# A transformer block in fp32: score beats paced by a weighted measure, and attention cut 5, 4 and 3 units ahead

## The chip, the cores and the metric

The kernel is one program on one core of a Trainium2 chip. The metric is device time in microseconds (us) of one launch, lower is better. Five engines work side by side, each through its own queue in order: PE (TensorE, matmuls), DVE (VectorE), ACT (ScalarE), POOL (GpSimd) and SP (SyncE, which here only issues DMAs). Semaphores tie them together: an instruction that waits holds up everything behind it on its engine.

## The reference

One pre-norm transformer layer in fp32 on x of shape (2, 1024, 1024), 32 heads of 32, feed-forward width 2752:

```python
def attn(x):
    qkv = x @ attn_qkvw + attn_qkvb            # q, k, v: 32 heads of 32
    scores = einsum('bhqd,bhkd->bhqk', q, k) / sqrt(32)
    ctx = einsum('bhqk,bhkd->bhqd', softmax(scores), v)
    return ctx @ attn_ow + attn_ob

def ffn(x):
    return (silu(x @ W_gate.T) * (x @ W_up.T)) @ W_down.T

x = x + attn(layernorm(x))
x = x + ffn(layernorm(x))
```

## The kernel before

**Stages.** There are two batches (b) and two blocks of 512 tokens in each (blk), so four blocks. The program is one long list of steps, nearly all of them one matmul each on PE:

- a head: layer norm, transposes and the first projections (`ln1`, `qk_steps`, `v_steps`);
- the fill: the remaining q, k and v projections of both batches (L370 and L432 are their matmuls);
- four times a rest (`rest(n)`), one for each block: the output projection (`oproj_steps`, matmul L770) with the second layer norm, then the feed-forward (`ffn_steps`): 22 chunks of gate and up products (`product`, matmul L912, a Strassen scheme of seven products), and after every fourth chunk a down projection.

A down projection (`down7`, matmul L1053, 28 matmuls of 512 columns) is again a Strassen scheme: each of its 14 accumulators in PSUM is added by DVE into one or two quarters of the residual x (L1066, L1068), 20 such adds in all, and DVE forms four sums of the hidden activations in between (`sums_h`, L1022 to L1028). The last, shorter part of a block uses `down` (matmul L985, add L996, and the regroupings `release`, L1010 and L1011). PSUM accumulators of all these, and the small transposes of attention, rotate through one pool of three buffers (tag `lin`).

**Attention.** It runs beside these steps in 64 units of two heads and 512 queries (`Unit`), 16 for each block. A unit has eight key tiles. Two key tiles at a time are scored by PE (`scores`, matmul L510) into two PSUM buffers (tag `s`, two of them). ACT copies each score tile to SBUF (L529), DVE keeps a running maximum over them (L526, one buffer `top`). After the eighth tile, DVE transposes and reduces the maximum (L549, L550), PE turns it (L564), DVE finishes it (L565), and DMAs through DRAM broadcast it to a tile m. Then for each key tile POOL subtracts the maximum (`less_maximum`, L580; every fourth on DVE in the first 16 units), ACT takes the exponential (L586), POOL or DVE adds neighbours (`add`, L596), and PE multiplies with the values (`values`, matmul L608), eleven beats or more after the score. The finished context goes to DRAM, and its softmax sums come back for a reciprocal on DVE (L696). Before the output projection of a block, POOL multiplies the context by these reciprocals (L718, waiting for the DMA of `rec`) and adds the bias to x (L762).

**What sets the order.** All instructions are written out in the order in which `Emitter.run` takes steps. It has a list `fill` (the projections, or a rest) and a list `paced` (attention). Each attention step with `beat=True` is a beat, eight for each unit, and every second one carries a pair of score tiles. A beat is held back until `due`, and `due` moves on by the work left divided by the beats left:

```python
                each = left / beats
                due = max(due, self.clock - each) + each
```

So beats lie evenly over the planned cost (`MM4 = 855.0` for one matmul of 512 columns) of the work in that call. If `fill` is not ready, `paced` goes on without regard to `due`. Steps with a delay (`em.later`) are written out when the planned clock has passed.

`attention_steps(cuts)` cuts the whole attention list, 512 beats and a drain of 14, into four lists. `lists[0]` is run beside the fill, `lists[1]` to `lists[3]` beside the rests of blocks 0 to 2; block 3 has none. Cuts stand at beats 144, 272 and 400: the fill takes the 16 units of the first block and two more, each later list 16 units. A rest keeps its last 30 matmuls (`late`) for the next call. On the side run the reloading of contexts (`prep_ctx`) and, during the fill, sums of weights on POOL (`weight_sum_steps`, L1164).

Of the kernel before, what the change touches and what calls it, by code (L numbers as in the profile page):

```python
# [24 lines left out]
class Steps:  # L25
# [3 lines left out]
    def __init__(self):  # L29
        self.items = []  # L30

    def add(self, fn, cost=0.0, needs=None, gives=None, beat=False):
        self.items.append((fn, cost, needs, gives, beat))

    def slack(self, cost):

# [2 lines left out]
    @property  # L39
    def cost(self):  # L40
        return sum(i[1] for i in self.items)


class Emitter:
# [21 lines left out]
    def run(self, fill, paced=None, side=()):  # L66

        paced = Steps() if paced is None else paced  # L70
        left = fill.cost + paced.cost
        beats = sum(i[4] for i in paced.items)
        due = self.clock

        def ready(q):
            return q.items and (q.items[0][2] is None or q.items[0][2] in self.done)

        while fill.items or paced.items:
            q = next((q for q in side if ready(q)), None)
            if q is None:  # L80
                go = ready(paced)
                if go and paced.items[0][4] and self.clock < due and ready(fill):
                    go = False
                q = paced if go else fill if ready(fill) else None
            if q is None:
                waiting = [p for p in self.put_off if p is not None]
                assert waiting, ("the steps wait for each other", fill.items[:1], paced.items[:1])
                self.clock = min(p[0] for p in waiting)
                self.settle()
                continue  # L90
            fn, cost, needs, gives, beat = q.items.pop(0)
            if beat:
                each = left / beats
                due = max(due, self.clock - each) + each
                beats -= 1
            fn()
            self.clock += cost
            if q is fill or q is paced:
                left -= cost
            if gives is not None:  # L100
                self.done.add(gives)
            self.settle()
# [28 lines left out]
def preln_block_kernel(  # L131
# [15 lines left out]
    B, S, H = x.shape  # L147
    G = w_qk.shape[0]
    KC = H // P
    NT = S // P  # L150
    NS = S // NH
# [7 lines left out]
    SCALE = 1.0 / math.sqrt(HD)  # L159
    MM4, MM1 = 855.0, 230.0  # L160
    UNITS = HEADS // 2
    QTR = 4
    LAG = 3
    RUN = 4
# [300 lines left out]
    class Unit:  # L465
# [4 lines left out]
        def __init__(self, n):  # L470
            self.n = n
            self.phase, u = divmod(n, UNITS)
            self.b, self.blk = divmod(self.phase, NS)
# [119 lines left out]
        def add(self, kt):  # L593

            eng = nc.vector if self.phase == 0 or kt % RUN == RUN - 1 else nc.gpsimd
            eng.tensor_tensor(self.p[kt], self.p[kt], self.p[kt - 1], ALU.add)  # L596
# [27 lines left out]
        def finish(self):  # L624
            part, n = divmod(self.u, UNITS // QTR)
            cs = Sm(f"cs_{self.name}")
# [11 lines left out]
    def attention_steps(cuts):  # L638


        units = [Unit(n) for n in range(B * NS * UNITS)]
        lists = [Steps()]
# [194 lines left out]
    def ffn_steps(q, b, blk, st, turn):  # L837
# [212 lines left out]
        def down7(pi, n, t, j):  # L1050
            if j == 0:
                st["pd"] = lps(f"pd{n}_{b}_{blk}_{pi}_{t}")
            nc.tensor.matmul(  # L1053
                st["pd"],
                lefts[n](pi)[:, j, t * P : (t + 1) * P],
                st["wp", pi, n, j],
                start=(j == 0),
                stop=(j == PART // 2 - 1),
            )
            if t == 1:  # L1060
                dst.next()
            if j == PART // 2 - 1:
                for (u, hf), op in goes[n]:
                    xs = st["x", t + u][:, hf * NH : (hf + 1) * NH]
                    if op == ALU.add:
                        nc.vector.tensor_tensor(xs, st["pd"], xs, op)  # L1066
                    else:
                        nc.vector.tensor_tensor(xs, xs, st["pd"], op)  # L1068

        def down_steps(pi):  # L1070
            if pi < WHOLE:
                for n in order:
                    for t in range(2):
                        for j in range(PART // 2):
                            q.add(lambda n=n, t=t, j=j: down7(pi, n, t, j), MM4)
                    if n in (1, 2, 4, 7):
                        q.add(lambda i=(1, 2, 4, 7).index(n): sums_h(pi, i))
                return


            for hf in range(NHF):
                for t in range(TB):
                    for ci in range(len(parts[pi])):
                        q.add(lambda hf=hf, t=t, ci=ci: down(pi, hf, t, ci), MM4)
                    if hf == 0 and t < 2:
                        q.add(lambda t=t: release(t))

# [100 lines left out]
    with tc.manual_schedule():  # L1188

        head, fill, keep_qk = Steps(), Steps(), Steps()  # L1190

        def two(fn, *args, **kw):

            q = Steps()
            fn(q, *args, **kw)
            return q

        def ln_steps(q, b, t0, t1, tools, ahead):

            load, norm, turn, _ = tools  # L1200
            for t in range(t0, t1):
                if t + ahead < t1:
                    q.add(lambda t=t + ahead: norm(t))
                turn(q, t)
                if t + 5 < NT:
                    q.add(lambda t=t + 5: load(t))

        tools = load, norm, turn, _ = ln1(0)
        for t in range(4):
            head.add(lambda t=t: load(t))  # L1210
        head.add(lambda: nc.sync.dma_start(bqk_t, b_qk))
        for _ in range(4):
            head.add(wst.next)
        head.add(lambda: load(4))
        for _ in range(8):
            head.add(dst.next)
        for _ in range(5):
            head.add(wst.next)
        head.add(lambda: norm(0))
        ln_steps(head, 0, 0, TB, tools, 1)  # L1220
        for _ in range(2):
            head.add(dst.next)
        qk_steps(head, 0, 0, [0])
        head.add(lambda: norm(TB))
        side = two(ln_steps, 0, TB, NT, tools, 1)
        head.items += merged(two(v_steps, 0, 0, range(TB)), side).items
        qk_steps(head, 0, 0, [1])

        v_steps(fill, 0, 0, range(TB, NT))
        for g in range(1, G // 2):  # L1230
            qk_steps(fill, 0, g)
        v_steps(fill, 0, 1)
        for g in range(G // 2, G - 2):
            qk_steps(fill, 0, g)

        tools = load1, norm1, turn1, stats1 = ln1(1)
        for t in range(5):
            fill.add(lambda t=t: load1(t))
        qk_steps(fill, 0, G - 2, [0])
        fill.items += merged(two(qk_steps, 0, G - 1, [0]), stats1(0, TB)).items  # L1240
        last = two(qk_steps, 0, G - 2, [1])
        qk_steps(last, 0, G - 1, [1])
        fill.items += merged(last, two(ln_steps, 1, 0, TB, tools, 1)).items
        fill.items += merged(two(v_steps, 1, 0, range(2)), stats1(TB, TB)).items
        fill.items += merged(
            two(v_steps, 1, 0, range(2, TB)), two(ln_steps, 1, TB, NT, tools, 1)
        ).items
        v_steps(fill, 1, 0, range(TB, NT))
        for g in range(0, G // 2):
            qk_steps(fill, 1, g)  # L1250
        v_steps(fill, 1, 1)
        for g in range(G // 2, G - 2):
            qk_steps(fill, 1, g)
        for s in range(NS):
            for g in range(G - 2, G):
                qk_steps(keep_qk, 1, g, [s])
            if s == 0:
                keep_qk.add(lambda: None, gives=("half", 1))

        def rest(n):  # L1260

            q, late, st = Steps(), Steps(), {}
            b, blk = divmod(n, NS)
            turn = oproj_steps(q, b, blk, st)
            ffn_steps(q, b, blk, st, turn)
            while late.cost < 30 * MM4:
                late.items.insert(0, q.items.pop())
            return q, late


        rests = [rest(n) for n in range(B * NS)]
        lists = attention_steps([(n + 1) * UNITS * NT + 2 * NT for n in range(B * NS - 1)])
        side = [*prep_ctx(0), *prep_ctx(1)]
        em.run(head)
        em.run(fill, lists[0], side=(*side, weight_sum_steps()))
        keep = keep_qk
        for (q, late), beats in zip(rests, [*lists[1:], None]):
            em.run(joined([keep, q]), beats, side=side)
            keep = late
        em.run(keep)  # L1280
        em.settle(True)
# [51 lines left out]
```

## Time and profile before

| | us |
|---|---|
| median of 3 runs (lowest, highest) | 3324.98 (3316.03, 3329.62) |
| the profiled execution's own time | 3320.48 |
| span of its trace | 3318.7 |
| PE busy | 3231.4 (97%) |
| DVE busy | 1904.9 (57%) |
| POOL busy | 1704.9 (51%) |
| ACT busy | 1431.9 (43%) |

Times below are us from the start of the span. The head and the fill end near 904; the rests of the four blocks follow. The matmuls of the last block's output projection begin at 2860.20, and beside it runs no attention. PE is busy nearly all the time, so time is lost where PE waits or where its clock is reduced: the list of waits (who waited for whom: total us, times, longest us), the table of windows (busy us and number of instructions of each engine in a stretch, PEclk being the granted share of PE's clock) and the timeline (start, length, instruction, and in brackets the idle time before it) are the views to read. The idle time of the other engines costs nothing by itself.

### The profile page before, as it was taken

How to read it: one execution, taken by the hardware profiler on the slowest of the kernel's cores; microseconds unless marked ns; L12 is line 12 of the kernel's file. 1: busy time of each engine (PE TensorE's matmuls, PEld its weight loads, DVE VectorE, ACT ScalarE, POOL GpSimd, SP SyncE). 2: the span in 40 equal slices, each digit the busy share in tenths (PEclk: the TensorE clock that was granted, in tenths of full speed). 3: DMA queues.
4: the chain of work that ended last, by engine and by line, in shares of the span. 5: the costliest groups of instructions: out<-in, count | busy, mean ns of one | idle time of the engine just before them, and what ended most of it. 6: DMA issues, size and time to landing. Idle time of an engine off the chain costs nothing. (4 is left out here: it accounts for less than half of the span.)

```text
span 3318.7 us, 44204 instructions
## 1 busy us (share of the span) xinstructions
PE 3231.4 (97%) x16576; PEld 1807.2 (54%) x16576; DVE 1904.9 (57%) x2462; ACT 1431.9 (43%) x1570; POOL 1704.9 (51%) x839
## 2 busy tenths in 40 slices
PE   8999999999999999998999999989999999999999
PEld 4444444444346555663465556634656566476775
DVE  2255565454366666667666676676666664344434
ACT  2244554444455555553555555545655554010000
POOL 0266666765675555557755565667665665200000
PEclk9999999999999999999999999999999999999999
DMA  4566666554534445546344454563454544544552
GB/s 154 173 184 203 211 197 208 187 178 137 148 101 139 146 146 147 148 142 199 103 134 144 138 143 136 149 179 118 135 145 145 146 139 138 177 145 152 154 153 95
DMA packets 337252, 507.33 MB, mean 153 GB/s; under 512 B 105360, under 2 KB 122000, under 8 KB 337040
## 3 DMA queue, kind: packets, MB, share of 16 engines
q1 hardware_dynamic: 280848, 405.91, 41.1%
q10 hardware_dynamic: 56192, 98.60, 9.8%
q8 instruction: 132, 2.16, 0.3%
q14 instruction: 80, 0.66, 0.1%
HBM read 429.14 MB, written 75.24 MB: 152 GB/s over the span
## 5 line engine op out<-in xcount | busy, mean ns | idle before, releaser
L580 POOL TENSOR_TENSOR p<-p,m 128x1024 f32<-128x1024 f32 x480 | 1172.0, 2464 | 27.3 <-DMA m<-d 27.2
L529 ACT COPY p<-s 128x1024 f32<-128x1024 f32 x512 | 516.6, 1012 | 908.1 <-DVE top L526 682.8
L526 DVE TENSOR_TENSOR top<-s,top 128x1024 f32<-128x1024 f32 x384 | 468.3, 1220 | 318.7 <-PE s L510 308.6
L912 PE MATMUL p<-sum,m 128*128 128x256 f32 x2688 | 619.7, 383 | 11.6 <-DVE gate L928 6.8
L586 ACT ACTIVATE p<-p 128x1024 f32<-128x1024 f32 x512 | 531.0, 1057 | 194.3 <-POOL p L580 177.7
L596 POOL TENSOR_TENSOR p<-p,p 128x1024 f32<-128x1024 f32 x96 | 227.6, 2371 | 678.7 <-ACT p L586 644.7
L912 PEld LDWEIGHTS p<-sum,m 128*128 128x128 f32 x2688 | 503.4, 190 | 133.2 <-issue 43.0
L912 PE MATMUL p<-xn2T,m 128*128 128x256 f32 x2016 | 473.1, 383 | 2.2 <-ACT gate L924 1.3
L370 PE MATMUL pq<-xnT,wqk 128*128 128x512 f32 x1024 | 465.2, 602 | 0.0
L1053 PE MATMUL pd<-wp,h 128*128 128x512 f32 x960 | 440.8, 605 | 11.4 <-DVE x L1066 10.9
L912 PEld LDWEIGHTS p<-xn2T,m 128*128 128x128 f32 x2016 | 377.6, 191 | 99.1 <-issue 45.1
L596 DVE TENSOR_TENSOR p<-p,p 128x1024 f32<-128x1024 f32 x160 | 273.0, 1706 | 121.7 <-ACT p L586 121.5
L370 PEld LDWEIGHTS pq<-xnT,wqk 128*128 128x128 f32 x1024 | 187.7, 191 | 253.6 <-issue 251.3
L1053 PEld LDWEIGHTS pd<-wp,h 128*128 128x128 f32 x960 | 178.3, 192 | 245.2 <-issue 207.0
L510 PE MATMUL s<-q,k 32*128 32x512 f32 x2048 | 298.6, 642 | 11.2 <-ACT p L529 11.2
L1066 DVE TENSOR_TENSOR x<-pd,x 128x512 f32<-128x512 f32 x360 | 236.8, 681 | 90.8 <-PE pd L1053 90.6
L608 PE MATMUL acc<-p,vals 128*32 128x256 f32 x4096 | 271.4, 382 | 3.5 <-DVE p L596 3.5
L1164 POOL TENSOR_TENSOR ws<-raw 128x512 f32<-128x512 f32 x62 | 88.5, 1428 | 337.7 <-DMA raw<-in_w_gu 184.1
L432 PE MATMUL pvv<-wv,xnT 128*128 128x512 f32 x512 | 232.9, 599 | 1.1 <-ACT xnT L266 1.1
L770 PE MATMUL po<-wo,ctx 128*128 128x512 f32 x512 | 231.8, 601 | 0.0
L608 PEld LDWEIGHTS acc<-p,vals 128*32 128x32 f32 x4096 | 119.8, 109 | 145.0 <-issue 71.2
L975 POOL MEMSET h<- 64x512 f32 x4 | 2.1, 518 | 340.9 <-PE pd L1053 340.9
(95 smaller groups left out, 2507.6 us busy)
## 6 DMA issues: line engine op xcount, KB each, us to landing
m<-dws SPq DMA_DIRECT2D x336, 256.0 KB
m<-in_w_gu SPq DMA_DIRECT2D x252, 256.0 KB
wp<-ddn SPq DMA_DIRECT2D x160, 256.0 KB
m<-d SPq DMA_DIRECT2D x64, 512.0 KB
wp<-in_w_dn SPq DMA_DIRECT2D x120, 256.0 KB
raw<-in_w_gu ACTq DMA_DIRECT2D x84, 256.0 KB
dws<-ws ACTq DMA_DIRECT2D x84, 256.0 KB
x<-in_x SPq DMA_DIRECT2D x32, 512.0 KB
```

What stands on the lines that cost most here:

```text
L370: nc.tensor.matmul(ps, wqk[b, g, w, hk][:, k, :], xnT[b, s][:, kc, :], start=(kc == 0), stop=(kc == KC - 1),)
L432: nc.tensor.matmul(st["ps"], xnT[b, t // TB][:, kc, (t % TB) * P : (t % TB + 1) * P], st["w"][kc], start=(kc == 0), stop=(kc == KC - 1),)
L510: nc.tensor.matmul(ps[a][:, h * NH : (h + 1) * NH], self.k[rows, i * P : (i + 1) * P], self.q[rows, :], start=True, stop=True,)
L526: nc.vector.tensor_tensor(self.top, s, self.p[0] if kt == 1 else self.top, ALU.max)
L529: nc.scalar.copy(self.p[kt], s)
L580: eng.tensor_tensor(p, p, self.m, ALU.add)
L586: nc.scalar.activation(self.p[kt], self.p[kt], AF.Exp, scale=SCALE)
L596: eng.tensor_tensor(self.p[kt], self.p[kt], self.p[kt - 1], ALU.add)
L608: nc.tensor.matmul(self.acc[j * HD : (j + 1) * HD, c : c + NQ], w(h), self.p[kt][:, q0 : q0 + NQ], start=start, stop=stop, skip_group_chec ...
L912: nc.tensor.matmul(ps, mats[c, n][:, kc, :], rhs, start=(kc == 0), stop=(kc == hk - 1),)
L1053: nc.tensor.matmul(st["pd"], lefts[n](pi)[:, j, t * P : (t + 1) * P], st["wp", pi, n, j], start=(j == 0), stop=(j == PART // 2 - 1),)
L1066: nc.vector.tensor_tensor(xs, st["pd"], xs, op)
```

## The change

Each step gets a factor `pace`, and the pacing of beats goes by the cost times this factor (`measure`, `now`) in place of the planned clock. The factor is 1 for all steps but the matmuls of both kinds of down projection, which get `DOWN = 0.3`: beside them, beats are spaced 1/0.3 times as wide in planned cost, and beside all other steps a little closer, since the number of beats in a list is spread over a smaller sum. The cuts of the attention list move to beats 168, 288 and 408: the fill takes 21 units in place of 18, the later lists 15 units each (the last one its remainder).

```diff
-    def add(self, fn, cost=0.0, needs=None, gives=None, beat=False):
-        self.items.append((fn, cost, needs, gives, beat))
+    def add(self, fn, cost=0.0, needs=None, gives=None, beat=False, pace=1.0):
+        self.items.append((fn, cost, needs, gives, beat, pace))
...
+    @property
+    def measure(self):
+        return sum(i[1] * i[5] for i in self.items)
...
-        left = fill.cost + paced.cost
+        left = fill.measure + paced.measure
...
-        due = self.clock
+        now = due = 0.0
...
-                if go and paced.items[0][4] and self.clock < due and ready(fill):
+                if go and paced.items[0][4] and now < due and ready(fill):
...
-            fn, cost, needs, gives, beat = q.items.pop(0)
+            fn, cost, needs, gives, beat, pace = q.items.pop(0)
             if beat:
                 each = left / beats
-                due = max(due, self.clock - each) + each
+                due = max(due, now - each) + each
                 beats -= 1
...
             if q is fill or q is paced:
-                left -= cost
+                left -= cost * pace
+                now += cost * pace
...
+    DOWN = 0.3
...
-                            q.add(lambda n=n, t=t, j=j: down7(pi, n, t, j), MM4)
+                            q.add(lambda n=n, t=t, j=j: down7(pi, n, t, j), MM4, pace=DOWN)
...
-                        q.add(lambda hf=hf, t=t, ci=ci: down(pi, hf, t, ci), MM4)
+                        q.add(lambda hf=hf, t=t, ci=ci: down(pi, hf, t, ci), MM4, pace=DOWN)
...
-        lists = attention_steps([(n + 1) * UNITS * NT + 2 * NT for n in range(B * NS - 1)])
+        ahead = (5, 4, 3)
+        lists = attention_steps([((n + 1) * UNITS + a) * NT for n, a in enumerate(ahead)])
```

## The prediction

> **What bounds the kernel now.** The page comes first, then the chain of waits from its end: both say PE.
>
> ```profile
> PE 3231.4 (97%) x16576; PEld 1807.2 (54%) x16576; DVE 1904.9 (57%) x2462; ACT 1431.9 (43%) x1570; POOL 1704.9 (51%) x839
> ```
>
> ```profile
> 2979.26 24.03 PE pd L1053 x56
> 3003.29 48.35 PE p L912 x224
> ```
>
> The second fence is the chain in the last block, where no attention runs: a down projection alone takes 24.03 us, four chunks of gate and up 48.35, and all of them repeat to 0.01 us. The change removes no matmul and adds none, so it can only win back time in which PE waits or is slow. How much is there? The waits of PE over the whole span (line and tile waiting, line and tile waited for, total us, times, longest):
>
> ```profile
> PE top L564 <- DVE part L550: 13.0, 7, 3.2
> PE pd L1053 <- DVE x L1066: 11.5, 13, 4.6
> PE s L510 <- ACT p L529: 11.2, 5, 4.4
> PE pt_a L258 <- ACT x L247: 10.2, 4, 7.8
> PE p L912 <- DVE gate L928: 6.8, 3, 4.2
> PE pd L985 <- DVE x L1066: 4.5, 1, 4.5
> ```
>
> All rows of this answer add up to 82 us; the fourth is the head and untouched. So some 70 us, 2% of the time, is the most there is, plus what the clock adds. Where it lies is read by asking the same waits for each stage, beside the table of windows (busy us of PE, PEld, DVE, ACT, POOL, then PEclk):
>
> ```profile
> 1528.00:1561.00 33.00, 24.86 (x107) 9.81 (x106) 28.02 (x24) 13.74 (x15) 31.02 (x14) 0.90 0.62 183
> 1644.00:1739.00 95.00, 88.00 (x570) 63.37 (x563) 62.93 (x82) 54.52 (x61) 58.38 (x27) 0.98 0.48 134
> 1739.00:2203.00 464.00, 449.57 (x2614) 269.13 (x2613) 307.99 (x407) 239.81 (x255) 267.12 (x125) 0.99 0.50 144
> 2203.00:2234.00 31.00, 23.55 (x107) 9.18 (x106) 26.44 (x24) 13.62 (x15) 29.32 (x13) 0.94 0.59 184
> ```
>
> The first and last row are the last short down projection of blocks 0 and 1 with the start of the next output projection: PE is busy 25 of 33 and 24 of 31 us, and the granted clock dips to 0.90 and 0.94, which costs another 0.10 x 33 = 3.3 and 0.06 x 31 = 1.9 us. The second row is the first gate and up stretch of block 1, the third its rest. How a wait beside a down projection comes about shows in the timeline (PE, then DVE):
>
> ```profile
> 2054.04 1.14 PE L510 MATMUL s<-q,k 32*128 32x512 f32 x8
> 2057.76 0.33 PE L564 MATMUL top<-ident,part 128*128 128x128 f32 x1 [2.59 <-DVE part L550]
> ...
> 2051.02 2.81 DVE L942 TENSOR_TENSOR h<-gate,up 128x512 f32<-128x512 f32 x1 [1.60 <-ACT gate L940]
> 2056.29 0.70 DVE L549 STREAM_TRANSPOSE m<-top 128x512 f32<-128x512 f32 x1
> 2057.02 0.69 DVE L550 TENSOR_REDUCE part<-m 128x16 f32<-128x512 f32 x1
> ```
>
> PE reaches the turn of a maximum at 2055.2 and DVE, behind with the work of the down projection, delivers at 2057.7. The four matmuls behind it wait too. At the block's end it is ACT that is late: its copy of a score tile stands behind an exponential that waits for POOL (ACT waits 15.3 us for L580 between 1520 and 1562), and POOL for the DMA of the reciprocals.
>
> **Part 1, beats spaced wider beside the down projections.** The counts come from the order in which PE's instructions stand in the two built programs. Beside the first four down projections of blocks 0 to 2 (twelve in all) stood 37 score pairs, 19 groups of value matmuls and 11 turns; now 13, 8 and 8. DVE's own work in one is 20 adds of 0.68 us, four sums (0.71, 0.93, 0.98, 1.41) and one product h (1.22), 18.9 us. Attention added to each 37/12 pairs x 2.44 (two maxima of 1.22), 19/12 adds x 1.71 and 11/12 maxima x 3.05 (two transposes of 0.70, two reductions of 0.69, one of 0.27), 13.0 us. That is 31.9 us for DVE, against 24.0 + 3.1 x 1.14 + 1.6 x 2.72 = 31.8 for PE (2.72 is a value group in the timeline): DVE has no slack. Now 18.9 + 2.6 + 1.1 + 2.0 = 24.6 against 27.1: a slack of 2.5 us. So the change relieves DVE, but by less than the pairs suggest, because PE's stretch shrinks too.
>
> What lies there is 3.6 us of waits (1085 to 1528), 14.5 less one of 4.6 that belongs to part 2 (1739 to 2203), and 2.1 (2409 to 2844, without the 4.5 below): 15.6, and some 3 of clock. The waits for x adds (6.9) should fall with the pairs, by two thirds, 4.6. The waits of turns (6.8) lose 3 of 11 turns, 1.9, and a third of the rest, 1.6. Not more, since in block 0 a turn now stands near the end of each of these down projections, where DVE is latest. Half of the clock's share, 1.5. **-10 us**; bounds 0 (the turns meet DVE as late as before) and -19 (all gone).
>
> **Part 2, the ends of blocks 0 and 1.** Beside the fifth and the last down projection stood 12 pairs, now 6, and the two turns beside the last one are gone. Waits there: 8.2 and 7.4 in the two windows above and the 4.6 before the second, 20.2, with 6.8 of clock. Score waits behind ACT (4.4 and 2.8) halve with the pairs, 3.6. The two turns (2.7 each) go, 5.4. The waits for adds (1.1 and 1.9) halve, 1.5. The 4.6 began with a reciprocal that waited 3.8 us for its DMA on DVE. That wait only moves to an earlier place, into the gate and up work, where the gate adds are late next: a quarter, 1.2. A third of the clock, 2.3. **-14 us**; bounds -5 (POOL's queue, next section) and -25.
>
> The wait of 4.5 at the end of block 2 stays: the last unit's values stand beside the same matmuls in both programs, and its sums still come back by the same DMA. So does everything behind it.
>
> **Part 3, what is moved elsewhere.** 30 pairs left the down projections: 13 are in the fill (the three units), 10 in later gate and up stretches, 4 in the three first ones, 3 in the output projections.
>
> - *Fill:* 80 pairs become 93. It waits 7.5 us after the head. In proportion that gives 1.2 more; with POOL also summing weights I take **+3**; bounds -2 (waits fall elsewhere) and +8 (one more wait of the size of the 3.1 for ACT's projections and its kin).
> - *First gate and up stretches:* 26 pairs become 30, 16 us more for DVE (4.06 a pair with its share of maxima and adds) against 10 for PE, where DVE is busy 63 of 95 us and PE waits 6.5, 7.1 and 4.5 for it. **+4**; bounds 0 and +10.
> - *Later gate and up stretches:* no wait of L912 there at 75 pairs; at 85, nothing. The cover is PSUM's three buffers. If it fails, it costs what the first stretches lose.
> - *Output projections:* 24 pairs become 27. POOL needs 6.3 us for each ((8 x 2.46 + 2 x 2.37 + 0.86)/4). **+2**; bounds 0 and +8.
> - *Switches:* PE's runs of one kind go from 1007 to 1018, and a matmul before a score or value group takes 523 ns from start to start, not 429. **+1**.
>
> The moved units bring their DMAs along: q and k on ACT's queue, values, d2 and m on SP's. None of the waits of PE above ends on one of these, and a beat in the fill still has at least (904 + 34)/168 = 5.6 us in place of 904/144 = 6.3 (34 is 13 pairs of 1.14 and 7 value groups of 2.72 more): nothing.
>
> Sum: -10 - 14 + 3 + 4 + 2 + 1 = **-14 us**. On the profiled execution's own 3320.5 that is 3306, -0.42%; that execution lies 4.5 us below the median and inside the three runs.
>
> **A rule weighed.** Row first: after the wait of 2.59 us above, the window 2052 to 2064 has a granted clock of 0.86, that is 1.7 us lost in 12; so a wait of that size is paid with two thirds again. The Trainium skill ("TensorE: Matmul & The Clock Gate", section "HAM oscillation — how this bites in real kernels") warns only of idle gaps over about 3.4 us. By that rule the waits of part 1, all shorter, would cost no clock, and the sum would be -12.5. The row decides, since 2.59 is below the rule's gap.
>
> **Rivals.**
>
> 1. *Both stretches come clean.* DVE's new slack ends all waits of parts 1 and 2: 19 + 27 less the 10 of part 3 gives -36, 3285. For it: the down projections of the last block, without attention, show 24.03 each time. Against: eight turns and the POOL queue remain.
> 2. *Slower: POOL falls behind in the output projection.* `paced` runs ahead when the output projection waits for its contexts, so after the last L718 ten subtractions, eight bias adds and two adds follow each other, 10 x 2.46 + 8 x 1.33 + 2 x 2.37 = 40 us, beside some 31 us of PE's work as the instructions stand. The window 2234 to 2314 has POOL busy 60.56 of 80 and waiting 8.8 for x. With one more pair it is 67 + 9 of 83. It decides once the DMA waits in this stretch grow by the 7 us left: then values wait about 8 us and the clock takes 1.7, in three places, 29, and some 3 more in the fill. With -14: +18, 3338. Against: PE waits only 0.5 us for values there now.
> 3. *The waits only change place*, because beats still fall into step with the chunks: 0, 3320.
>
> **Numbers.** A measurement of this kernel can tell about 0.5%, 17 us, from no change. Forecast 0.58, with its own range of -27 to -2: of it 0.24 lies beyond 17 us and 0.34 within. Rival 1: 0.17, faster. Rival 2: 0.15, of it 0.13 slower and 0.02 within. Rival 3: 0.10, within. So faster 0.41, same 0.46, slower 0.13. The bounds of the parts add up to -45 and +22. The range leaves out a tenth on each side: -36 (rival 1's figure) to +16.
>
> **What would show it.** Right: at the ends of blocks 0 and 1, two windows of the same work with PE waiting under 4 us each and a granted clock near 1; waits "top <- part" down from 13 to about 6; no change in the last block. Wrong: "acc <- p" among PE's longest waits (rival 2), waits of L912 for gate adds well over 12 us, or turns waiting 2 us in each down projection of block 0 (rival 3).

## The result, and the profile after

The changed kernel takes 3345.99 us (median of 8 runs, 3332.86 to 3359.56) against 3321.82 for the kernel before (8 runs, 3316.03 to 3329.62): ratio 1.0072, 95% interval 1.0054 to 1.0091. It is slower by 24 us, where the forecast was 14 faster. The profiled execution has an own time of 3348.9 and a span of 3347.1 (before: 3320.48 and 3318.7), so the two traces show the difference in full, and 4 us more than the medians do. Lines of the changed kernel lie 6 higher than before: L510 is now L516, L596 is L602, L1053 is L1059, L1066 is L1072.

The page's first row, and the chain of waits in the last block:

```profile
PE 3246.5 (97%) x16576; PEld 1808.7 (54%) x16576; DVE 1926.5 (58%) x2462; ACT 1425.3 (43%) x1569; POOL 1722.1 (51%) x839
```

```profile
3008.65 24.03 PE pd L1059 x56
3032.68 48.35 PE p L918 x224
```

The same 16576 matmuls, and the block without attention repeats to the 0.01 us. For the same work PE is busy for 15 us longer, and it is idle for 13 more. Where, the list of PE's waits tells (line and tile waiting, line and tile waited for, total us, times, longest):

```profile
PE pd L1059 <- DVE x L1072: 19.2, 22, 2.9
PE acc L614 <- DVE p L602: 15.3, 7, 5.3
PE pt_a L264 <- ACT x L253: 11.0, 4, 7.7
PE top L570 <- DVE x L1072: 7.6, 9, 1.4
PE top L570 <- DVE part L556: 5.2, 2, 3.0
PE pvv L438 <- DVE xnT L270: 4.3, 1, 4.3
PE pt_a L264 <- DVE vv L450: 4.3, 1, 4.3
```

What was to shrink did: "top <- part" went from 13.0 to 5.2, "s <- p" from 11.2 to 1.4. The first row grew from 11.5 in 13 waits, though beats beside the down projections became fewer. Besides it stand waits that before were small or absent: values for the neighbour adds (second row), turns for a PSUM buffer that an x add has yet to free (fourth), and two waits in the fill (the last two). The second and the fourth row, as they were before the change:

```profile
PE acc L608 <- DVE p L596: 3.5, 2, 3.0
PE top L564 <- DVE x L1066: 0.7, 2, 0.4
```

Four windows: the last short down projection of block 0; the first gate and up stretch of block 1; the rest of block 1; its end, that is the fifth and the last down projection (columns as before: busy us of PE, PEld, DVE, ACT, POOL, then PEclk):

```profile
1587.44:1603.60 16.16, 16.16 (x49) 6.43 (x47) 11.68 (x15) 3.94 (x4) 12.77 (x7) 1.00 0.84 269
1694.00:1800.00 106.00, 96.92 (x626) 66.54 (x625) 70.23 (x93) 62.27 (x70) 65.66 (x31) 0.94 0.44 129
1800.00:2211.00 411.00, 403.82 (x2358) 250.53 (x2355) 264.15 (x359) 212.68 (x227) 231.80 (x105) 1.00 0.48 142
2211.00:2262.00 51.00, 45.56 (x163) 18.41 (x162) 38.30 (x46) 12.29 (x13) 31.51 (x18) 1.00 0.70 215
```

The first row has PE busy all the time at full clock, where 25 of 33 us were busy at 0.90 before: that part of the change works, with two score pairs beside it and no turn. The second is worse than its counterpart: 9.1 us not busy and 0.94, against 7.0 and 0.98.

**Where the 28 us went.** To compare stages of different content, each stage is charged with its loss: its real length in the trace, less the length that its PE instructions have at their undisturbed pace from start to start (a matmul before another, before a score group and so on). Each row comes from one profiled execution. The fill, whose order is the same in the changed kernel and in after_no_bias and add_pool (experiments below) up to the seventeenth unit, has lost up to 9 us more in one than in another by 600 us; differences of that size in a single column are noise. For ends_three the profiled execution was the slowest of four (3290.69). The last block is equal in all. The column "fill" is the delay that has built up at the last two groups of q and k projections (some 10 us of it are the head's); "ends" are the fifth and the last down projection of blocks 0 to 2, "downs" the first four of each.

| kernel | time, ratio to before | fill | output projections | first gate/up | later gate/up | downs | ends |
|---|---|---|---|---|---|---|---|
| before | 3321.82 | 11.8 | 10.5 | 20.5 | -0.1 | 30.5 | 39.6 |
| changed | 1.0072 | 33.2 | 17.2 | 34.2 | 6.2 | 36.7 | 13.9 |
| difference | | +21 | +7 | +14 | +6 | +6 | -26 |
| pace_only | 1.0044 | 14.2 | 25.1 | 30.3 | 10.0 | 23.3 | 21.3 |
| ahead_only | 1.0042 | 35.3 | 11.8 | 19.7 | 0.8 | 22.9 | 35.7 |
| mid_only | 1.0136 | 7.9 | 39.0 | 34.1 | 11.1 | 22.2 | 38.3 |
| ends_only | 0.9913 | 8.3 | 2.9 | 22.0 | 1.5 | 29.6 | 14.1 |
| ends_tenth | 0.9999 | 8.2 | 25.5 | 19.7 | 2.2 | 38.5 | 8.7 |
| ends_half | 1.0046 | 9.5 | 20.1 | 37.6 | 3.2 | 31.3 | 18.0 |
| ends_three | 0.9889 | 10.6 | 3.7 | 19.6 | 0.0 | 25.3 | 21.5 |

The differences add up to 28 us, the difference of the spans. In the other rows up to 8.5 us are left over (for pace_only the columns give 11 us more than before, the spans 20): what is lost behind the last projections, at the very end of the fill, stands in no column.

**The fill.** Timeline of the changed kernel, PE, then DVE, then POOL, where the layer norm of the second batch meets attention:

```profile
467.56 5.33 PE L438 MATMUL pvv<-wv,xnT 128*128 128x512 f32 x6 [4.34 <-DVE xnT L270]
```

```profile
459.88 2.59 DVE L586 TENSOR_TENSOR p<-p,m 128x1024 f32<-128x1024 f32 x1
462.40 3.37 DVE L602 TENSOR_TENSOR p<-p,p 128x1024 f32<-128x1024 f32 x1
465.70 1.21 DVE L532 TENSOR_TENSOR top<-s,top 128x1024 f32<-128x1024 f32 x1
466.83 0.67 DVE L270 COPY xnT<-pt_a 128x512 f32<-128x512 f32 x1
```

```profile
459.04 5.65 POOL L586 TENSOR_TENSOR p<-p,m 128x1024 f32<-128x1024 f32 x2
```

PE waits for a copy of 0.67 us. It stands on DVE behind a subtraction and an add that last 2.59 and 3.37 us; both kinds take 1.21 when they run alone. POOL works through two subtractions in just that time. The same happens at 510, for the next 4.33.

**The output projection.** Block 1, POOL, DVE, PE:

```profile
1639.95 9.29 POOL L586 TENSOR_TENSOR p<-p,m 128x1024 f32<-128x1024 f32 x4
```

```profile
1640.80 9.52 DVE L602 TENSOR_TENSOR p<-p,p 128x1024 f32<-128x1024 f32 x1
```

```profile
1650.38 1.08 PE L614 MATMUL acc<-p,vals 128*32 128x256 f32 x8 [5.25 <-DVE p L602]
```

One add on DVE, 1.21 us of work, lasts as long as a row of four POOL subtractions and ends 1.1 us after them. The values wait 5.25 us for it. In the other two output projections such waits come to 4.4 (two of them) and 2.8 us.

**The down projections of block 0.** PE near the end of one of them, and the clock behind it:

```profile
1268.81 1.12 PE L1059 MATMUL pd<-wp,h 128*128 128x512 f32 x2 [0.53 <-DVE x L1072]
1271.35 0.48 PE L570 MATMUL top<-ident,part 128*128 128x128 f32 x1 [1.41 <-DVE x L1072]
```

```profile
1271.30:1274.70 3.40, 3.35 (x5) 1.53 (x6) 2.60 (x4) 0.00 (x0) 0.00 (x0) 0.50 0.26 77
```

The turn of a maximum stands behind 22 to 24 of the 28 matmuls of the down projection, in all four of block 0 (25 to 27 us after its start in the trace), and needs a buffer that DVE, late with its x adds, has not freed. Two waits of 0.53 and 1.41 us are followed by 3.4 us at half clock.

### The profile page after: what moved, and what is told of

The parts are those of the page before. It is cut to its first block, busy times and chain, and to the rows that moved or that the text cites. A ratio compares the mean times of both kernels' runs of the same rounds, so it can differ in the third digit from the quotient of the medians.

```text
span 3347.1 us, 44194 instructions
## 1 busy us (share of the span) xinstructions
PE 3246.5 (97%) x16576; PEld 1808.7 (54%) x16576; DVE 1926.5 (58%) x2462; ACT 1425.3 (43%) x1569; POOL 1722.1 (51%) x839
## 4 chain that ended last, share of the span: by engine, by line
PE 53%; DVE 8%; issue 2%; ACT 2%; POOL 1%; DMA 1%; SPq 0%; ACTq 0%; DVEq 0%; POOLq 0%
PE p L918 26%; PE pd L1059 11%; PE acc L614 6%; PE po L776 4%; PE s L516 4%; PE pd L991 1%; DVE top L532 1%; DVE x L1072 1%; DVE p L602 1%; POOL p L586 1%; DVE m L555 1%; DVE h L948 1%; PE pg L962 0%; DVE part L556 0%; ACT p L535 0%
## 5 line engine op out<-in xcount | busy, mean ns | idle before, releaser
L586 POOL TENSOR_TENSOR p<-p,m 128x1024 f32<-128x1024 f32 x480 | 1181.7, 2485 | 13.3 <-DMA m<-d 7.1
L918 PE MATMUL p<-sum,m 128*128 128x256 f32 x2688 | 626.7, 384 | 10.9 <-DVE gate L934 5.1
L602 POOL TENSOR_TENSOR p<-p,p 128x1024 f32<-128x1024 f32 x96 | 228.3, 2378 | 745.9 <-ACT p L592 730.5
L1059 PE MATMUL pd<-wp,h 128*128 128x512 f32 x960 | 435.5, 603 | 18.3 <-DVE x L1072 17.7
L1059 PEld LDWEIGHTS pd<-wp,h 128*128 128x128 f32 x960 | 179.9, 192 | 251.6 <-issue 201.4
L516 PE MATMUL s<-q,k 32*128 32x512 f32 x2048 | 300.1, 642 | 1.6 <-ACT p L535 1.4
L602 DVE TENSOR_TENSOR p<-p,p 128x1024 f32<-128x1024 f32 x160 | 281.8, 1761 | 24.6 <-ACT p L592 24.6
L1072 DVE TENSOR_TENSOR x<-pd,x 128x512 f32<-128x512 f32 x360 | 237.0, 682 | 99.7 <-PE pd L1059 99.4
```

Source lines behind the costliest of these rows:

```text
L516: nc.tensor.matmul(ps[a][:, h * NH : (h + 1) * NH], self.k[rows, i * P : (i + 1) * P], self.q[rows, :], start=True, stop=True,)
L586: eng.tensor_tensor(p, p, self.m, ALU.add)
L918: nc.tensor.matmul(ps, mats[c, n][:, kc, :], rhs, start=(kc == 0), stop=(kc == hk - 1),)
L1059: nc.tensor.matmul(st["pd"], lefts[n](pi)[:, j, t * P : (t + 1) * P], st["wp", pi, n, j], start=(j == 0), stop=(j == PART // 2 - 1),)
```

## The experiments

**The two halves of the change.** One has the pace alone, with the old cuts; one the cuts alone, with pace 1.

```diff
 pace_only
-        ahead = (5, 4, 3)
+        ahead = (2, 2, 2)
 ahead_only
-    DOWN = 0.3
+    DOWN = 1.0
```

> The spacing of 0.3 beside the down projections with the cuts of before (18 units in the fill). Theory A (three prices that add up: +22 us in the fill from the three units, -26 at the block ends from the spacing, +27 elsewhere from the pairs that the spacing pushes into the first gate and up stretches and the output projections): the fill as before, the ends -20 to -26, the rest +15 to +30, so -10 to +10 us in all, and values waiting for DVE adds in the output projections as in the changed kernel. Rival B (the moved cuts alone cost, the spacing helps): -15 to -25 us.

> The cuts 5, 4 and 3 units ahead with even spacing (factor 1). Theory A: the fill is the same list as in the changed kernel and shows the same +20 us or so; the rests carry 15 units in place of 16 at even spacing and lose nothing or win a little (0 to -8), so +12 to +22 us. Rival B: +30 to +50 us, since the cuts also bring the losses in the first gate and up stretches and the output projections.

pace_only: 3332.57 us, 1.0044 (1.0028 to 1.0059). ahead_only: 3334.11, 1.0042 (1.0028 to 1.0057). The pace costs more than theory A's -10 to +10, the cuts what it gave. Each costs some 14 us, and together they give the change's loss. The table puts the price of the cuts into the fill (35.3) and that of the pace into the output projections and gate and up stretches (25.1, 30.3, 10.0), which the cuts alone leave as they were.

**The two parts of the pace.** With the old cuts, the factor is given to the fifth and last down projections only, or to the first four of each block only.

```diff
 ends_only
-        ahead = (5, 4, 3)
+        ahead = (2, 2, 2)
-                            q.add(lambda n=n, t=t, j=j: down7(pi, n, t, j), MM4, pace=DOWN)
+                            q.add(lambda n=n, t=t, j=j: down7(pi, n, t, j), MM4, pace=DOWN if pi == WHOLE - 1 else 1.0)
 mid_only
-        ahead = (5, 4, 3)
+        ahead = (2, 2, 2)
-                            q.add(lambda n=n, t=t, j=j: down7(pi, n, t, j), MM4, pace=DOWN)
+                            q.add(lambda n=n, t=t, j=j: down7(pi, n, t, j), MM4, pace=DOWN if pi < WHOLE - 1 else 1.0)
-                        q.add(lambda hf=hf, t=t, ci=ci: down(pi, hf, t, ci), MM4, pace=DOWN)
+                        q.add(lambda hf=hf, t=t, ci=ci: down(pi, hf, t, ci), MM4)
```

> The cuts of before, and the spacing of 0.3 only beside the fifth and the last down projection of each block. Theory A: most of the ends' win (-15 to -25) with little pushed elsewhere (+3 to +8): -8 to -20 us. Rival C (waits move with the accidental alignment of units and chunks, and no stage has a price of its own): within 5 us of before, or a loss elsewhere of the size of the win.

> The cuts of before, spacing of 0.3 only beside the first four down projections of each block, not beside the fifth and the last. Theory A, now from two runs (spacing everywhere +12 us, spacing at the ends alone -29): spacing beside the four middle ones costs some +25 to +40 us by itself, most of it outside the down projections (first gate and up stretches, later gate and up stretches, output projections: +20 or more against before together), while the twelve down projections win at most 10. Rival D (spacing is good everywhere, and what cost was the start of block 0's rest): -10 to +5 us.

ends_only: 3290.38, 0.9913 (0.9898 to 0.9928): 29 us faster, more than expected. mid_only: 3363.30, 1.0136 (1.0121 to 1.0151): 44 slower, a little above what was expected. So the pace is two changes of opposite sign; their ratios add up to +0.49%, and pace_only has +0.44%. From the lists of PE's waits, three rows of ends_only, then two of mid_only:

```profile
PE s L516 <- ACT p L535: 3.4, 1, 3.4
PE top L570 <- DVE part L556: 3.0, 3, 1.4
PE acc L614 <- DVE p L602: 2.1, 1, 2.1
```

```profile
PE s L516 <- ACT p L535: 21.9, 8, 6.1
PE acc L614 <- DVE p L602: 13.5, 5, 5.8
```

In mid_only the down projections win 8 us and everything that got their beats loses: output projections +28, gate and up +14 and +11.

**How many units ahead.** fill_three has pace 1 and one more unit in the fill than before (`ahead = (3, 3, 3)`), fill_four two more (`(4, 3, 3)`). shift_half is the changed kernel with 20 and a half units in the fill; it also takes the turns of block 0 away from the ends of its down projections.

```diff
 shift_half
-        ahead = (5, 4, 3)
-        lists = attention_steps([((n + 1) * UNITS + a) * NT for n, a in enumerate(ahead)])
+        ahead = (4.5, 4, 3)
+        lists = attention_steps([int(((n + 1) * UNITS + a) * NT) for n, a in enumerate(ahead)])
```

> Even spacing (factor 1), all cuts 3 units ahead in place of 2: one unit more in the fill, not three. Theory A: a third of the fill's price, +5 to +9 us there, and about that in all. Rival C: no proportion; anything from -5 to +20 us in the fill.

> Even spacing, cuts 4, 3 and 3 units ahead: two units more in the fill. One more cost the fill nothing (2.1 us of loss against 2.3), three more cost 21 to 23. Density (DVE runs out of slack beside the second batch's layer norm): 3 to 14 us in the fill, between the two. Alignment: 0, or over 20.

> The changed kernel with the first cut half a unit earlier (20.5 units in the fill, block 0's attention shifted by half a unit against its chunks; blocks 1 and 2 keep their order). In the changed kernel the turn of a maximum stands 22 to 24 us into each of block 0's first four down projections, which lost 17.7 us together; here none of them holds a turn. If the turns are what costs there: 4 to 8 us for the four. If the beats or DVE's load cost there: 14 us or more. The fill should lie between the runs with 20 and 21 units: 11 to 24 us over before.

fill_three: 3320.56, 1.0009 (0.9996 to 1.0022), no difference, where theory A gave +5 to +9. fill_four: 3342.02, 1.0074 (1.0059 to 1.0089). shift_half: 3323.69, 1.0022 (1.0009 to 1.0035). The delay at the end of the fill is 7.9 to 14.2 us with 18 units (eight kernels), 10.6 and 11.6 with 19, 22.7 with 20, 27.5 with 20 and a half, 33.2 to 35.3 with 21 (three kernels): free up to 19, then some 11 us a unit. In add_pool, a fourth kernel with 21, it is larger still, by some 9 us more than in the changed kernel.

In shift_half the first four down projections of block 0 lose 2.9 us in place of 17.7. PE's waits in 1147 to 1552, changed kernel, then shift_half, the rows for x adds:

```profile
PE pd L1059 <- DVE x L1072: 5.0, 8, 0.9
PE top L570 <- DVE x L1072: 4.3, 4, 1.4
```

```profile
PE pd L1059 <- DVE x L1072: 2.4, 2, 2.2
PE top L570 <- DVE x L1072: 1.5, 2, 1.2
```

The four turns that waited in step with the chunks are gone, and the two half-clock stretches at 1271 and 1370 us with them. Score pairs (4 and 5) and value groups (4 and 3) beside these down projections are nearly the same in both, so the turns are what differs. It is not the place near the end alone: in blocks 1 and 2 of the changed kernel two down projections have a turn behind 10 or 11 of their 28 matmuls, and each of them loses some 4 us too. fill_four lost more than the 11 us of that column: up to the end of the fill it is 20 us behind before (among them a wait of 6.3 us for a score tile that ACT copies), and its profiled execution is 18 us longer as a whole. It is slower than ahead_only, which has one unit more in the fill: the whole time does not go by the number of units.

**What delays DVE in the fill.** five_no_sums is ahead_only without the sums of weights on POOL.

```diff
 five_no_sums
-            ws = Hs(f"ws{i}")
+            ws = raw
...
-                nc.gpsimd.tensor_tensor(out_, in0, in1, op)
+                pass
...
-                nc.scalar.dma_start(out_[:, j, :], ws[:, j, :])
+                nc.scalar.dma_start(out_[:, j, :], raw[:, j, :])
```

> Cuts 5, 4 and 3 with even spacing, and the sums of weights left out on POOL (the raw weights are stored in their place, so the products use other numbers): 124 POOL operations of 1.4 us less during the fill. If POOL's operations hold up DVE's operations with two SBUF inputs, those take near 1.2 us in the fill in place of 2.0 to 2.4, DVE is no longer late beside the second batch's layer norm, and the fill's waits behind DVE (4.3, 5.6 and 1.2 us) go: 15 us or more less in the fill. If DVE is late from its own load alone, they stay.

One run: 3309.02, with a fill delay of 18.8 in place of 35.3. Two rows of PE's waits in the fill of ahead_only, then three of five_no_sums:

```profile
PE pt_a L264 <- DVE vv L450: 5.6, 1, 5.6
PE pvv L438 <- DVE xnT L270: 4.3, 1, 4.3
```

```profile
PE s L516 <- ACT p L535: 8.0, 3, 7.0
PE pvv L438 <- DVE xnT L270: 2.2, 1, 2.2
PE pt_a L264 <- DVE vv L450: 1.3, 1, 1.3
```

In the fill, DVE's adds and subtractions with both inputs in SBUF last 78.6 us longer in all than 1.21 each in ahead_only and in the changed kernel, 50.9 before, 68.2 in fill_four, and 42.9 here. So the sums on POOL make up 36 us of this excess, and without them the waits behind DVE shrink and 16.5 us of the fill's loss go. The excess is not the whole of it: five_no_sums has less than the kernel before (42.9 against 50.9) and still loses 7 us more in the fill, and its longest wait there, 7.0 us, is for a score tile that ACT copies. Nor do the operations fall to 1.2 us, as was expected: 0.4 us each stay, with POOL's subtractions still running beside them.

**Adds on POOL.** add_pool is the changed kernel with all neighbour adds of the units from the seventeenth on put on POOL, so that DVE's late adds can't hold the values.

```diff
 add_pool
-            eng = nc.vector if self.phase == 0 or kt % RUN == RUN - 1 else nc.gpsimd
+            eng = nc.vector if self.phase == 0 else nc.gpsimd
```

> The changed kernel with all neighbour adds of units 16 and later on POOL (before and in the changed kernel every second one of them is DVE's). In the output projections PE waited for a DVE add that ran 6.9, 9.5 and 7.1 us beside a row of POOL operations in place of 1.2. If DVE is held up by POOL's operations: no DVE operation over 4 us there, and the output projections lose 0 to 8 us in place of 17. If POOL's queue itself is late: they lose 15 to 30, with values waiting for POOL adds, and the time grows by 5 to 20 us.

3341.07, 1.0062 (1.0048 to 1.0076): not to be told from the changed kernel's 1.0072, where 5 to 20 us more were expected if POOL's queue is late. No add or subtraction on DVE lasts over 3.4 us there. But the output projections lose more (25.3), with the waits now on POOL's own adds:

```profile
PE acc L614 <- POOL p L602: 11.7, 5, 3.5
```

So with these adds on it POOL's queue itself is late; a DVE add held by its row is one form of the same.

**The best parts together, and the factor.** ends_three is ends_only with the cuts of fill_three; ends_tenth and ends_half are ends_only with 0.1 and 0.5 for 0.3.

> Spacing of 0.3 at the ends alone, all cuts 3 units ahead. One more unit in the fill cost nothing and spacing at the ends won 29 us; if the two add up, 3285 to 3293. If a shift by one unit moves the waits again: 3295 to 3315.

> As the run with spacing at the ends alone, but 0.1 in place of 0.3. If the ends' stalls are already gone at 0.3 (14 us left there of 40, the rest not from attention), 0.1 changes nothing: within 5 us of 3290. If beats there still cost: 3280 to 3286. If the pairs pushed out cost elsewhere: 3295 to 3305.

> Spacing at the ends alone, 0.5 in place of 0.3. 0.1 piled beats up in the output projections (25 us there, 9 at the ends), 0.3 did not (3 and 14). If the price is a smooth sum of the two: 3290 to 3302. If 0.3 is a lucky alignment: over 3305.

ends_three: 3282.75, 0.9889 (0.9874 to 0.9904), the fastest here, faster than the kernel before and the changed one; its interval touches that of ends_only, so the one unit more is not shown to help. ends_tenth: 3320.79, 0.9999 (0.9984 to 1.0015). ends_half: 3335.49, 1.0046 (1.0033 to 1.0058). ends_tenth lies above all three of its figures, and ends_half meets the condition that was set for it: 0.3 is a lucky alignment. With 0.1, 0.3 and 0.5 the ends themselves lose less than before (8.7, 14.1, 18.0, against 39.6), and that much follows the spacing; what differs is the output projections behind them, 25.5, 2.9 and 20.1, and in ends_half the first gate and up stretches. The two kernels with 0.3 at the ends are faster, but no rule for spacing the ends follows from them.

**Is it POOL in the output projection?** POOL's work there, counted in the programs with the durations of before, is 77 to 82% of the undisturbed length in the three output projections of before, 82 to 86% in ends_only, 87% in blocks 1 and 2 of ends_tenth, 91% in ends_half, 88 to 89% in the changed kernel and 83 to 92% in mid_only. These are counts of what stands in the program there. In time, the windows of the three output projections show POOL busy 72 to 77% in the changed kernel and 74 to 77% before, probably because work that comes late falls into the next stage. The share alone does not decide: shift_half, with the changed kernel's order in blocks 1 and 2 and 88%, loses only -0.2 and 2.0 us there, against 6.5 and 5.6. So three kernels (the changed one, ends_half and mid_only) leave out the bias in each output projection, eight adds of 1.33 us on POOL, with the order of everything else kept:

```diff
 after_no_bias, half_no_bias, mid_no_bias
-                    nc.gpsimd.tensor_tensor(xs, xs, st["bo", hf], ALU.add)
+                    pass
```

> The changed kernel without the bias of the output projection (POOL's eight adds of 1.33 us in each output projection are left out, all else in the same order). POOL's work there falls from 73.5 to about 63 us of 83.5 undisturbed. If POOL's queue is what delays the values (DVE's neighbour adds held by its rows included), the loss in the three output projections falls from 17 to under 6 us, waits of acc on p from 15 to under 5, and the time by 8 to 16 us, to 3330 to 3338. If it is the alignment of DVE and ACT with the matmuls, the loss stays within 4 of 17 and the time within 5 of the changed kernel's 3346. The losses in the fill (22 more than before) and in the first gate and up stretches (14 more) stay in both cases.

> The ends paced by 0.5, also without the bias of the output projection. POOL's work in the output projections of blocks 1 and 2 falls from 91% of the undisturbed length to 78%. POOL's queue as the cause: the loss of 20 us there falls under 6, the time from 3335 to 3315 to 3325; the 38 us in the first gate and up stretches may fall too, if they begin with what the output projection left late (then towards 22, and the time under 3310). Alignment: 15 us or more stay in the output projections, the time over 3328.

> Pace on the first four down projections only, also without the bias of the output projection. It lost 39 us in the output projections, most of all kernels. POOL's queue as the cause: under 12 left, the time from 3363 to 3330 to 3342. Score tiles that wait for ACT at the ends on their own account, independent of POOL: 25 or more left there, the time over 3350.

| | time | ratio (95%) | output projections, with bias and without | first gate/up |
|---|---|---|---|---|
| after_no_bias | 3331.73 | 1.0031 (1.0016, 1.0047) | 17.2 to -1.3 | 34.2 to 34.5 |
| half_no_bias | 3316.59 | 0.9990 (0.9978, 1.0001) | 20.1 to 6.0 | 37.6 to 37.7 |
| mid_no_bias | 3356.92 | 1.0114 (1.0092, 1.0135) | 39.0 to 24.7 | 34.1 to 32.8 |

In the changed kernel the whole loss of the output projections goes, and "acc <- p" leaves the head of the list of PE's waits, while the rows of the down projections stay:

```profile
PE pd L1059 <- DVE x L1072: 19.2, 23, 2.9
...
PE top L570 <- DVE x L1072: 7.6, 9, 1.4
```

POOL's queue is the cause there, and of most of the loss in ends_half. Leaving out the bias also takes away POOL's waits for the transfer of x (0, 2.1 and 5.8 us in the three output projections of the changed kernel); how much of the win is theirs was not taken apart. In mid_only POOL's queue is a good third; of what remains, the largest waits are for score tiles behind ACT ("s <- p", 10.2 us in the three output projections without the bias, 13.3 with it). That they come from the last down projection, still dense with beats just before, is likely but not tested. The losses of the first gate and up stretches do not come from the output projection: they stay in all three.

## Why the prediction was wrong, step by step

- **Part 3, what is moved elsewhere: the step that failed.** It priced the stages that receive the beats by the waits already seen there, +10 in all (its last term, the switches' +1, has no stage of its own); they measured +48.
  - *Fill:* +3 taken (bounds -2 and +8), +21 measured. The step scaled the waits of before with the number of pairs and looked for one more wait on PE. But the fill was free up to 19 units only. Beyond that DVE's two-input operations, stretched by POOL's, lose 68 to 79 us in place of 51, DVE falls behind, and the layer norm of the second batch, which PE waits for, stands in its queue. The row that gave warning was there: DVE's adds with a mean of 1.71 and a maximum of 11.35 us, for an operation whose minimum is 1.17. (The maximum itself stands in an output projection; in the fill of before these adds take 1.72 on average.) That excess is what more units raise.
  - *First gate and up stretches:* +4 taken (bounds 0 and +10), +14 measured. The sum "16 us more for DVE against 10 for PE" pointed the right way, but the step took less than the difference, though PE already waited for DVE there. The table's kernels point the same way: where DVE's work, counted as POOL's above, is 74 to 77% of the undisturbed length, one such stretch loses 7.5 us on average (16 stretches, 3.8 to 14.1), at 78 to 81% it loses 10.8 (11 stretches, 3.6 to 16.8). The cause was not tested by itself.
  - *Later stretches:* 0 taken, +6 measured. The waits for gate and up that the trace names in these windows come to 2.1 us only, so the cover that the step names, three PSUM buffers, mostly held; what makes up the rest is not shown.
  - *Output projections:* +2 taken, +7 measured, inside the bounds. POOL's share by the program rose from about 80 to 88%, and the run without bias, which takes the whole loss away, shows that POOL's queue is the term.
- **Part 1 failed too:** -10 taken, +6 measured, outside its bounds of 0 and -19. Blocks 1 and 2 lose 5 us less than before, block 0 11 more. The prediction saw that in block 0 "a turn now stands near the end of each of these down projections, where DVE is latest" and took its figure down for it, yet not below 0. shift_half shows that these four turns cost some 15 us: without them the part measures -9.
- **Part 2:** -14 taken for blocks 0 and 1, some -20 measured there: right in cause and inside its bounds. The other 6 of the -26 are the end of block 2, where the wait of 4.5 was said to stay (7.4 to 1.1 us of loss). That was a misreading: the last unit's values stand behind 12 of the 28 matmuls of the fifth down projection before and behind 7 now, and DVE's wait for the DMA of their sums fell from 7.98 to 1.33 us.
- **The rivals.** Rival 3's mechanism, beats in step with the chunks, came true in block 0. Rival 2 came nearest in time (3338) and names the right sign and, for the output projection, the right queue, with waits of 4.4, 5.3 and 2.8 where it said 8. But it is not the main loss: without it the changed kernel is still 1.0031, against a kernel before that keeps its bias. The range ended at 3336 because each term of part 3 was bounded by waits seen before, and none by the queue filling up.
- **The rule weighed.** The row held in kind: waits of 1 to 3 us can be paid in clock. Its price was read too high, since the window 2052 to 2064 holds a second wait of 0.86 us besides the 2.59. Here waits of 0.53 and 1.41 us, 1 us apart in the trace, were followed by 3.4 us at half clock, and all stretches at half clock add up to 69 us in the changed kernel, against 43 before. The Trainium skill's rule ("TensorE: Matmul & The Clock Gate", section "HAM oscillation — how this bites in real kernels"), which warns of gaps over about 3.4 us, would have priced these two waits at nothing.
- **Still open:** why the first gate and up stretches of ends_half lose 37.6 and those of ends_tenth, with the same share of DVE's work in blocks 1 and 2 (78 to 79%), 19.7; what sets the rest of the wait for ACT in mid_only; and why 0.3 at the ends leaves the output projections nearly free where 0.1 and 0.5 do not. No run takes these apart.

## What to carry to other kernels

Work taken out of one stage lands in others: before spreading it, add up each engine's work in the stages that receive it as a share of their undisturbed length, and treat a stage near its limit as full (here: output projections with 87% or more of POOL's work, most of which lost 5 us or more, though not those of shift_half; the fill beyond 19 units). Undo a compound change part by part: here one part alone was worth -0.9%, and the other two hid it. Then try its constant on both sides: at 0.1 and 0.5 the same part was worth nothing and +0.5%. A step that recurs with the same period as the work beside it should be looked for in the order of the program: four turns that each met a down projection cost some 15 us, and half a unit of shift took them out.

## What the hardware showed that was not expected

- A DVE operation with both inputs in SBUF, 1.21 us alone, can last through a whole row of POOL operations that follow each other without a gap: 9.52 us beside four of them, and up to 11.35 in the kernel before. Mostly it is held up by one, up to 3.4 us.
- Short waits of PE count together for its clock. In each of the 17 traces the clock changes only on a grid of windows of 3.41 us, and how long PE idles in one window goes with the clock of the next. Of 155 windows at full clock with 2.0 us or more of idle time in all, 154 were followed by half clock; from 1.75 to 2.0 us it was 31 of 63, below that 13 of 15962. In 23 of the 155 no single gap reached 1.75 us. The waits of 0.53 and 1.41 us above fell into one such window, with 1.90 us idle in all.
